# A two-layer graph attention kernel on one core: quarter-width value matmuls, and group ends on ScalarE and in transfers

## The chip, the core and the metric

The kernel runs on one core of a Trainium2 chip. A core has TensorE for matmuls (PE in the profile; its weight loads are PEld), VectorE (DVE), ScalarE (ACT), GpSimd (POOL) and SyncE (SP, which here only issues transfers). SBUF is the memory of the engines, 128 partitions wide; PSUM is where TensorE writes. The metric is the device time of one execution in microseconds (us), lower is better.

## What is computed

The input is x (4096 x 512) and an adjacency matrix adj (4096 x 4096), all in 32-bit floats. Cut to what matters:

```python
# layer 0
h = relu(layernorm(x))
e = (h @ edge_w) @ (h @ edge_w).T                # 4096 x 4096
edge_att = softmax(where(adj > 0, e, -9e15), axis=1)
x = x + adj * (softmax(h @ node_w, axis=0) * edge_att) @ (h @ weight) + bias
# layer 1: 8 heads of 64
h = relu(layernorm(x))
v = (h @ W.T + b).reshape(4096, 8, 64)
e = leaky_relu(src[:, None] + trg[None, :], 0.01) + adj     # for each head; src, trg: sums over v
x = x + (softmax(e, axis=-1) @ v)                # for each head, heads side by side
```

So adj is a mask in layer 0 and an addend to the scores in layer 1.

## The kernel before

**Layer 0** has three passes. The first makes the projections. The second makes the scores e once for each symmetric pair of blocks, writes them to a DRAM scratch e_d and keeps row maxima. The third, around which the change is made, runs over 8 blocks b of 512 output rows and, in each, 32 tiles m of 128 source rows: 256 steps. The order is written out by hand (`manual_schedule`): at each step the functions of a list are called with a lead in steps, `stages = ((load, 8), (turn, 3), (exps, 2), (weigh, 1), (gather, 0))`. Every engine works through its own instructions in the order in which they are written there.

- `load`: SP fetches scores (`et` or `eb`) and adjacency (`a`).
- `turn`: where the stored block is the mirrored one, TensorE transposes it (L271).
- `exps`: VectorE masks and subtracts (L279, L282, L283), ScalarE takes the exponential (L285).
- `weigh`: VectorE multiplies by adj (L291); GpSimd sums the denominators in racc (L301).
- `gather`: four matmuls (L324) add to four PSUM banks po0 to po3, one for each 128 rows of the block. There is one set of these banks.

At m = 0 `gather` also fetches four x tiles through SP and adds the bias on GpSimd (L311). At m = 31 it makes row sums by TensorE (L318), takes the reciprocal on VectorE (L320, L321), and after the last matmuls VectorE reads each po, scales it and adds x (L328); GpSimd's queue stores it to x1 in DRAM (L330).

**Between the layers** a pass over 32 row tiles makes v (`va`), the head projections and four tables of exponentials. The leaky exponential splits so that only a max or a relu of a row vector z and a column factor has to be taken for each pair; z is stored in DRAM (z_d) and read back broadcast to all partitions.

**Layer 1's main loop** runs over 8 groups i: 4 blocks of 1024 output rows (WL) times 2 sets of 4 heads (HG). In each group there are 32 tiles m of 128 source rows, again 256 steps. `stages = ((load, 3), (exps, 1), (weigh, 1), (factors, 2), (gather, 0))`.

- `load`: SP fetches adjacency, tile e, 512 KB; there are three buffers.
- `zload`: a broadcast row of z, 512 KB, on GpSimd's queue. There are six buffers and four z to a group. z3 and z0 are loaded with the first `load` of a group, z1 and z2 with its first `factors`, so at leads of 3 and 2 steps.
- `factors`: ScalarE makes e3 = exp(e + log factor) for head 3 (L474) and rl = relu(...) from z0 (L477).
- `exps`: ScalarE makes ex = exp(e) in PSUM (L465), in one buffer.
- `weigh`: VectorE makes the four products pr of 128 x 1024 in the order k = 3, 0, 1, 2 (L489, and L486 for k = 0). k = 3 uses e3 and the others use ex. GpSimd adds k = 3 to acc3 (L498), and an accumulating transfer adds k = 0 to acc0 or acc1 (L504).
- `gather`: TensorE multiplies values and products (L516) into four PSUM banks pv, two heads in a bank (64 partitions each), and sums the denominators of k = 1 and 2 into the bank dn, in quarters of 32 partitions (L522). An fp32 matmul is two MATMUL and two weight-load instructions in the profile.

At m = 31 ScalarE copies the four pv banks and dn to SBUF (L531, L532). `finish` is a generator: from step 3 of the next group on, one stretch of it runs after each step. It transposes denominators and takes reciprocals (L543, L544), sums acc by matmuls with ones (L553 to L556, copied at L558), and then, for each pair of 128-row tiles, fetches y from x1 through ScalarE's queue (L567), transposes the values (L572), scales and adds them on VectorE (L575, L577, L578) and stores the result through ScalarE's queue (L579).

Of the kernel before, what the change touches and what calls it, by code (L numbers as in the profile page):

```python
# [8 lines left out]
FP = mybir.dt.float32  # L9
AF = mybir.ActivationFunctionType  # L10
ALU = mybir.AluOpType
# [4 lines left out]
P = 128  # L16
# [12 lines left out]
def kernel(  # L29
# [27 lines left out]
    ident = const.tile([P, P], FP, name="ident")  # L57
# [4 lines left out]
    x1 = dram.tile([N, F], FP, name="x1")  # L62
    z_d = dram.tile([H * NT, P], FP, name="z_d")
# [27 lines left out]
    na = big.tile([P, NT], FP, name="na")  # L91
# [128 lines left out]
    with tc.tile_pool(name="c_e", bufs=9) as etp, tc.tile_pool(name="c_b", bufs=4) as ebp, tc.tile_pool(  # L220
# [12 lines left out]
        def rows_of(m):  # L233
            return slice(m * P, (m + 1) * P)
# [69 lines left out]
        def gather(b, m):  # L304
            if m == 0:
                blk[b][2] = [p_o.tile([P, F], FP, name=f"po{j}") for j in range(TB)]
                blk[b][3] = []
                for j in range(TB):
                    xt = iop.tile([P, F], FP, name="xt")
                    nc.sync.dma_start(xt, x[rows_of(b * TB + j), :])  # L310
                    nc.gpsimd.tensor_tensor(xt, xt, bias_b, ALU.add)  # L311
                    blk[b][3].append(xt)
            mb, racc, po, xts = blk[b]
            last = m == NT - 1
            if last:
                rs = p_r.tile([P, TB], FP, name="rs")
                for j in range(TB):
                    nc.tensor.matmul(rs[:, j:j + 1], racc[:, j * P:(j + 1) * P], ones, start=True, stop=True)  # L318
                sc = sp.tile([P, TB], FP, name="sc")
                nc.vector.reciprocal(sc, rs)  # L320
                nc.vector.tensor_tensor(sc, sc, na[:, b * TB:(b + 1) * TB], ALU.mult)  # L321
            w = at.pop((b, m))
            for j in range(TB):
                nc.tensor.matmul(po[j], w[:, j * P:(j + 1) * P], sup[:, m, :], start=(m == 0), stop=last)  # L324
            if last:
                for j in range(TB):
                    ot = iop.tile([P, F], FP, name="ot")
                    nc.vector.scalar_tensor_tensor(ot, po[j], sc[:, j:j + 1], xts[j],  # L328
                                                   op0=ALU.mult, op1=ALU.add)
                    nc.gpsimd.dma_start(x1[rows_of(b * TB + j), :], ot)  # L330

        stages = ((load, 8), (turn, 3), (exps, 2), (weigh, 1), (gather, 0))
        for s in range(-8, len(steps)):
            for f, ahead in stages:
                if 0 <= s + ahead < len(steps):
                    f(*steps[s + ahead])
    l0.close()


# [91 lines left out]
    WL = 1024  # L431
# [3 lines left out]
    with tc.tile_pool(name="e", bufs=3) as ep, tc.tile_pool(name="e3", bufs=2) as e3p, tc.tile_pool(  # L435
# [13 lines left out]
        def load(i, m):  # L449
            b, g = groups[i]  # L450
            e = ep.tile([P, WL], FP, name="e")
            nc.sync.dma_start(e, adj_t[m * P:(m + 1) * P, b * WL:(b + 1) * WL])
            ra[i, m] = e
            if m == 0:
                zload(i, 3)
                zload(i, 0)

        def zload(i, k):
            b, g = groups[i]
            zs_[i, k] = zp.tile([P, WL], FP, name="z")  # L460
            nc.gpsimd.dma_start(zs_[i, k], row_bcast(z_d, WL, (g * HG + k) * N + b * WL))

        def exps(i, m):
            x_ = p_x.tile([P, WL], FP, name="ex")
# [41 lines left out]
        def gather(i, m):  # L506
            b, g = groups[i]
            if m == 0:
                pv[i] = ([[p_v.tile([P, BL], FP, name=f"pv{c}{q}") for q in range(HV)] for c in range(2)],
                         p_v.tile([P, BL], FP, name="dn"))  # L510
            v, dn = pv[i]
            flags = dict(start=(m == 0), stop=(m == NT - 1))
            for c, pair in enumerate(((3, 0), (1, 2))):
                for q in range(HV):
                    for r, k in enumerate(pair):
                        nc.tensor.matmul(v[c][q][r * D:(r + 1) * D, :], va[:, m, g * HG + k, :],  # L516
                                         pr[i, m, k][:, q * BL:(q + 1) * BL], **flags)
            for k in (1, 2):
                d = d_m[:, g * HG + k, m:m + 1]
                for q in range(HV):  # L520
                    r = (k - 1) * 2 + q
                    nc.tensor.matmul(dn[r * Q:(r + 1) * Q, :], d.to_broadcast([P, Q]),  # L522
                                     pr[i, m, k][:, q * BL:(q + 1) * BL], **flags)
            for k in range(HG):
                pr.pop((i, m - 1, k), None)
            if m == NT - 1:
                os_ = [[osp.tile([P, BL], FP, name=f"os{c}{q}") for q in range(HV)] for c in range(2)]
                od = osp.tile([P, BL], FP, name="od")
                for c in range(2):
                    for q in range(HV):  # L530
                        nc.scalar.copy(os_[c][q], v[c][q])  # L531
                nc.scalar.copy(od, dn)  # L532
                late[i] = os_, od

        def finish(i):
            b, g = groups[i]
            os_, od = late.pop(i)
            rd = sp.tile([P, WT, HG], FP, name="rd")

            def dens(src, two):  # L540
                pt = p_t.tile([P, WT // HV, P], FP, name="pt")
                for j in range(WT // HV):
                    nc.tensor.transpose(pt[:, j, :], src[:, j * P:(j + 1) * P], ident)  # L543
                nc.vector.reciprocal(rd[:, :, two].rearrange("p (q j) k -> p j k q", q=HV),  # L544
                                     pt.rearrange("p j (k q d) -> p j k q d", k=2, q=HV)[:, :, :, :, 0])

            dens(od, slice(2, 4))
            yield

            ps = p_t.tile([P, BL], FP, name="pt")  # L550
            for q in range(HV):
                s = slice(q * BL, (q + 1) * BL)
                nc.tensor.matmul(ps[q * Q:(q + 1) * Q, :], ones, acc[i, 3][:, s], start=True, stop=True)  # L553
                r = HV + q
                nc.tensor.matmul(ps[r * Q:(r + 1) * Q, :], ones, acc[i, 0][:, s], start=True, stop=False)
                nc.tensor.matmul(ps[r * Q:(r + 1) * Q, :], ones, acc[i, 1][:, s], start=False, stop=True)  # L556
            oa = osp.tile([P, BL], FP, name="oa")
            nc.scalar.copy(oa, ps)  # L558
            yield
            dens(oa, slice(0, 2))  # L560
            yield
            for j in range(0, WT, 2):
                rows = slice(b * WL + j * P, b * WL + (j + 2) * P)
                y = iop.tile([P, 2, HG, D], FP, name="y")

                cols = slice(g * HG * D, (g + 1) * HG * D)
                nc.scalar.dma_start(y, x1[rows, cols].rearrange("(j p) (h d) -> p j h d", p=P, h=HG))  # L567
                pt = p_t.tile([P, 2, HG, D], FP, name="pt")
                for q in range(2):
                    for c in range(2):  # L570
                        s = (j + q) * P % BL
                        nc.tensor.transpose(pt[:, q, 2 * c:2 * c + 2, :].rearrange("p k d -> p (k d)"),  # L572
                                            os_[c][(j + q) * P // BL][:, s:s + P], ident)
                o = sp.tile([P, 2, HG, D], FP, name="o")
                nc.vector.tensor_tensor(o, pt, rd[:, j:j + 2, :].unsqueeze(3).to_broadcast([P, 2, HG, D]),  # L575
                                        ALU.mult)
                nc.vector.tensor_tensor(y[:, :, 0:3, :], y[:, :, 0:3, :], o[:, :, 1:4, :], ALU.add)  # L577
                nc.vector.tensor_tensor(y[:, :, 3, :], y[:, :, 3, :], o[:, :, 0, :], ALU.add)  # L578
                nc.scalar.dma_start(out[rows, cols].rearrange("(j p) (h d) -> p j h d", p=P, h=HG), y)  # L579
                yield  # L580

        stages = ((load, 3), (exps, 1), (weigh, 1), (factors, 2), (gather, 0))
        for s in range(-3, len(steps)):
            for f, ahead in stages:
                if 0 <= s + ahead < len(steps):
                    f(*steps[s + ahead])
            if s > NT and s % NT == 3:
                ending = finish(s // NT - 1)
            if s > NT and s % NT >= 3:
                next(ending, None)  # L590
        for _ in finish(len(groups) - 1):
            pass
# [34 lines left out]
```

## Time and profile before

| What | Value |
|---|---|
| median of 3 runs | 3289.96 us (3289.59 to 3289.97) |
| the profiled execution | 3290.54 us, span 3288.7 us, granted TensorE clock 0.981 |
| layer 0, first pass | until about 283 us |
| layer 0, second pass | about 284 to 741 us |
| layer 0, third pass (L324) | 760.1 to 1745 us |
| between the layers | 1745 to 1915 us |
| layer 1, main loop | 1915.1 to 3261.2 us |
| after the last product | 3261.2 to 3288.7 us |

The span is counted from the first to the last instruction of the program; the execution's own time has 1.8 us around it. Busy times of an engine are sums within a stretch. A number in brackets behind a line of the timeline is the time that the engine stood idle before it, with the instruction or transfer that ended it.

### The profile page before, as it was taken

The page shows a single profiled execution, that of the slowest core. Times are in us where ns is not written, and L with a number is a line of the kernel's source. Part 1 is how long each engine was busy: PE and PEld are TensorE (multiplying, and loading weights), DVE is VectorE, ACT ScalarE, POOL GpSimd, SP SyncE. Part 2 cuts the span into 40 slices and gives each one's busy share as a digit, 9 for nine tenths or more (in the row PEclk, how much of TensorE's full clock was granted, in tenths as well). Part 3 has the DMA queues.
Part 4 walks back from the last instruction along what each step waited for, and adds up shares of the span by engine and source line. Part 5 has one row for each costly group of instructions (what it writes and reads, how often), then busy time and mean ns, then how long its engine had stood idle before and what let it go on. Part 6 is the DMA issues. An engine that isn't in the chain of part 4 may idle for free.

```text
span 3288.7 us, 34545 instructions
## 1 busy us (share of the span) xinstructions
PE 3117.9 (95%) x11514; PEld 1291.8 (39%) x11514; DVE 2573.5 (78%) x3593; ACT 1195.6 (36%) x1417; POOL 1415.7 (43%) x1081
## 2 busy tenths in 40 slices
PE   8999999998999999999998869999999999999997
PEld 4554444444444444444444423232323232323332
DVE  3324777776667678788896599898989898999997
ACT  2211111111111111111113256565656666666664
POOL 0001111113434445445454546565656565655554
PEclk9999999998999999999999989999999999999999
DMA  2104666656444444454433179898988898989896
GB/s 74 39 20 158 225 219 229 223 182 211 142 141 155 142 157 159 141 163 157 147 107 103 36 188 223 228 218 225 219 224 217 222 223 224 222 227 219 227 221 161
DMA packets 239250, 577.07 MB, mean 175 GB/s; under 512 B 26048, under 2 KB 51936, under 8 KB 239072
## 3 DMA queue, kind: packets, MB, share of 16 engines
q1 hardware_dynamic: 163680, 357.76, 32.7%
q0 software_dynamic: 55680, 196.13, 26.9%
q10 hardware_dynamic: 19712, 20.98, 2.1%
q8 instruction: 90, 1.47, 0.2%
q14 instruction: 88, 0.72, 0.1%
HBM read 389.02 MB, written 51.53 MB: 134 GB/s over the span
## 4 chain that ended last, share of the span: by engine, by line
PE 62%; DVE 18%; issue 6%; ACT 6%; DMA 4%; POOL 2%; ACTq 0%; DVEq 0%; SPq 0%; POOLq 0%
PE po L324 26%; PE pe L180 14%; DVE pr L489 13%; PE pv L516 8%; ACT e L474 5%; PE ps L136 3%; PE pe L129 3%; PE dn L522 2%; DMA z<-z_d 2%; PE pd L382 2%; PE pt L271 2%; DMA y<-x 1%; POOL pr L387 1%; PE lg L139 1%; DVE d L283 1%
## 5 line engine op out<-in xcount | busy, mean ns | idle before, releaser
L516 PE MATMUL pv<-pr,va 128*64 128x512 f32 x4096 | 1025.2, 610 | 61.5 <-DVE pr L489 40.2
L324 PE MATMUL po<-sup,at 128*128 128x512 f32 x2048 | 915.2, 598 | 45.1 <-DVE at L291 45.1
L498 POOL TENSOR_TENSOR acc<-acc,pr 128x1024 f32<-128x1024 f32 x240 | 570.3, 2376 | 434.2 <-DVE pr L489 434.0
L489 DVE SCALAR_TENSOR_TENSOR pr<-z,g_m,ex 128x1024 f32<-128x1024 f32 x512 | 631.4, 1273 | 41.9 <-DMA z<-z_d 41.9
L516 PEld LDWEIGHTS pv<-pr,va 128*64 128x64 f32 x4096 | 359.4, 137 | 686.0 <-issue 378.7
L324 PEld LDWEIGHTS po<-sup,at 128*128 128x128 f32 x2048 | 380.2, 192 | 479.7 <-issue 403.7
L301 POOL TENSOR_TENSOR racc<-racc,ex 128x512 f32<-128x512 f32 x240 | 354.7, 1478 | 467.4 <-ACT ex L285 466.8
L285 ACT ACTIVATE ex<-d 128x512 f32<-128x512 f32 x256 | 161.3, 630 | 829.0 <-DVE d L283 829.0
L180 PE MATMUL pe<-he_t 128*128 128x512 f32 (+3 forms) x1152 | 455.8, 557 | 0.1
L465 ACT ACTIVATE ex<-e 128x1024 f32<-128x1024 f32 x256 | 263.1, 1028 | 456.6 <-DVE pr L489 356.9
L486 DVE SCALAR_TENSOR_TENSOR pr<-rl,gd_m,ex 128x1024 f32<-128x1024 f32 x256 | 326.0, 1274 | 29.1 <-ACT ex L465 29.1
L489 DVE SCALAR_TENSOR_TENSOR pr<-z,g_m,e 128x1024 f32<-128x1024 f32 x256 | 327.6, 1280 | 0.0
L477 ACT ACTIVATE rl<-z,ngd_m,d_m 128x1024 f32<-128x1024 f32 x256 | 314.1, 1227 | 26.9 <-DMA z<-z_d 26.9
L180 PEld LDWEIGHTS pe<-he_t 128*128 128x128 f32 x1152 | 212.9, 190 | 234.5 <-issue 222.5
L474 ACT ACTIVATE e<-e,ld_m 128x1024 f32<-128x1024 f32 x256 | 290.0, 1133 | 5.0 <-DMA z_d<-zs 5.0
L283 DVE TENSOR_TENSOR d<-d,mk 128x512 f32<-128x512 f32 x256 | 273.7, 1069 | 8.8
L522 PE MATMUL dn<-pr,d_m 128*32 128x512 f32 x2048 | 273.8, 607 | 0.0
L184 POOL DMA_DIRECT2D e_d<-es x144 | 79.2, 550 | 351.3 <-ACT es L183 345.8
L282 DVE TENSOR_TENSOR d<-pt,mb 128x512 f32<-128x512 f32 (+2 forms) x136 | 87.4, 643 | 172.6 <-PE pt L271 172.6
L183 ACT COPY es<-pe 128x512 f32<-128x512 f32 (+2 forms) x144 | 79.3, 551 | 376.2 <-PE pe L180 376.2
L504 POOL DMA_DIRECT2D acc<-pr x240 | 208.2, 868 | 5.0 <-DVE pr L486 4.0
L291 DVE TENSOR_TENSOR at<-ex,a 128x512 f32<-128x512 f32 x256 | 190.5, 744 | 0.5
(116 smaller groups left out, 2182.9 us busy)
## 6 DMA issues: line engine op xcount, KB each, us to landing
e<-in_adj_t_dram SPq DMA_DIRECT2D x256, 512.0 KB, 4.5
acc<-pr POOLq DMA_DIRECT2D x256, 512.0 KB, 4.9
a<-in_adj_t_dram SPq DMA_DIRECT2D x256, 256.0 KB, 3.4
ar<-in_adj_dram SPq DMA_DIRECT2D x120, 256.0 KB, 3.1
e_d<-es POOLq DMA_DIRECT2D x120, 256.0 KB, 2.8
ac<-in_adj_t_dram SPq DMA_DIRECT2D x112, 256.0 KB, 3.2
eb<-e_d SPq DMA_DIRECT2D x28, 1024.0 KB, 5.8
et<-e_d SPq DMA_DIRECT2D x112, 256.0 KB, 3.5
```

The costliest lines, as they stand in the source:

```text
L180: nc.tensor.matmul(pe[:, :w], he_t[:, k, rows], he_t[:, k, cols], start=(k == 0), stop=(k == KC - 1))
L283: nc.vector.tensor_tensor(d, d, mk, ALU.add)
L301: nc.gpsimd.tensor_tensor(racc, racc, e, ALU.add)
L324: nc.tensor.matmul(po[j], w[:, j * P:(j + 1) * P], sup[:, m, :], start=(m == 0), stop=last)
L465: nc.scalar.activation(x_, ra.pop((i, m)), AF.Exp)
L474: nc.scalar.activation(x_, ra[i, m], AF.Exp, bias=ld_m[:, h + 3, m:m + 1])
L477: nc.scalar.activation(r, zs_[i, 0], AF.Relu, bias=ngd_m[:, h, m:m + 1], scale=d_m[:, h, m:m + 1])
L486: nc.vector.scalar_tensor_tensor(w, rl.pop((i, m)), gd_m[:, h, m:m + 1], x_, op0=ALU.add, op1=ALU.mult)
L489: nc.vector.scalar_tensor_tensor(w, zs_[i, k], g_m[:, h + k, m:m + 1], e3.pop((i, m)) if k == 3 else x_, op0=ALU.max, op1=ALU.mult)
L498: nc.gpsimd.tensor_tensor(acc[i, 3], acc[i, 3], w, ALU.add)
L516: nc.tensor.matmul(v[c][q][r * D:(r + 1) * D, :], va[:, m, g * HG + k, :], pr[i, m, k][:, q * BL:(q + 1) * BL], **flags)
L522: nc.tensor.matmul(dn[r * Q:(r + 1) * Q, :], d.to_broadcast([P, Q]), pr[i, m, k][:, q * BL:(q + 1) * BL], **flags)
```

## The change

There are five parts.

- **Layer 0, block ends.** The x loads and bias adds move from m = 0 to m = 8. At m = 31 ScalarE copies each po bank to SBUF (`oc`). VectorE's reciprocal and the scale-and-add move into a new `finish`, called once a step after `weigh` in steps 2 to 5 of the next block; it works in place on oc in SBUF.
- **Value matmuls.** Each value matmul of 64 output partitions becomes two of 32, with the same products streamed to both.
- **z loads** move from GpSimd's queue to SP's, and z0 is loaded ahead of z3.
- **Layer 1, group ends.** dn is copied at the first stretch of `finish`, which now runs at step 0 of the next group. Steps 1 and 2 are left out as places for stretches. The copy of the ones-matmuls' sums gets its own stretch.
- **Output of layer 1.** Transposed values go one 128-row tile to a stretch. ScalarE scales each head's 64 columns from PSUM into o with a per-partition factor, in the order of heads. An accumulating transfer on GpSimd's queue adds x1 to o, and a store on SP's queue, one stretch later, writes it to the output. VectorE's three instructions and ScalarE's two transfers are gone.

```diff
@@ layer 0, third pass
             if m == 0:
...
                 blk[b][3] = []
+            if m == TB * 2:
...
             if last:
                 for j in range(TB):
-                    ot = iop.tile([P, F], FP, name="ot")
-                    nc.vector.scalar_tensor_tensor(ot, po[j], sc[:, j:j + 1], xts[j],
-                                                   op0=ALU.mult, op1=ALU.add)
-                    nc.gpsimd.dma_start(x1[rows_of(b * TB + j), :], ot)
+                    oc = iop.tile([P, F], FP, name="oc")
+                    nc.scalar.copy(oc, po[j])
+                    left.append((b * TB + j, oc, rs if j == 0 else None, xts[j]))
+        def finish():
+            t, oc, rs, xt = left.pop(0)
+            b, j = divmod(t, TB)
+            if j == 0:
+                sc = sp.tile([P, TB], FP, name="sc")
+                nc.vector.reciprocal(sc, rs)
+                nc.vector.tensor_tensor(sc, sc, na[:, b * TB:(b + 1) * TB], ALU.mult)
+                scale[b] = sc
+            nc.vector.scalar_tensor_tensor(oc, oc, scale[b][:, j:j + 1], xt, op0=ALU.mult, op1=ALU.add)
+            nc.gpsimd.dma_start(x1[rows_of(t), :], oc)
...
+                if f is weigh and left and s % NT > 1:
+                    finish()
@@ layer 1
+                zload(i, 0)
                 zload(i, 3)
-                zload(i, 0)
...
-            nc.gpsimd.dma_start(zs_[i, k], row_bcast(z_d, WL, (g * HG + k) * N + b * WL))
+            nc.sync.dma_start(zs_[i, k], row_bcast(z_d, WL, (g * HG + k) * N + b * WL))
...
-                        nc.tensor.matmul(v[c][q][r * D:(r + 1) * D, :], va[:, m, g * HG + k, :],
-                                         pr[i, m, k][:, q * BL:(q + 1) * BL], **flags)
+                        for c0 in range(0, D, Q):
+                            nc.tensor.matmul(v[c][q][r * D + c0:r * D + c0 + Q, :],
+                                             va[:, m, g * HG + k, c0:c0 + Q],
+                                             pr[i, m, k][:, q * BL:(q + 1) * BL], **flags)
...
-                nc.scalar.copy(od, dn)
-                late[i] = os_, od
+                late[i] = os_, dn
         def finish(i):
...
+            od = osp.tile([P, BL], FP, name="od")
+            nc.scalar.copy(od, dn)
+            yield
...
+            for t in range(WT + 3):
+                if 0 < t <= WT:
+                    if t % 2:
+                        o = iop.tile([P, 2, HG, D], FP, name="o")
+                    for r, k in enumerate(ORDER):
+                        nc.scalar.activation(o[:, (t - 1) % 2, k, :], pt[:, r, :], AF.Copy,
+                                             scale=rd[:, t - 1, r:r + 1])
+                    if t % 2 == 0:
+                        nc.gpsimd.dma_start(o, part(x1, b * WT + t - 2, cols), accum_op=ALU.add)
+                if t > 2 and t % 2:
+                    nc.sync.dma_start(part(out, b * WT + t - 3, cols), oo)
+                if t % 2 == 0:
+                    oo = o
+                if t < WT:
+                    q, j = divmod(t, WT // HV)
+                    pt = p_t.tile([P, HG, D], FP, name="pt")
+                    for c in range(2):
+                        nc.tensor.transpose(pt[:, 2 * c:2 * c + 2, :].rearrange("p k d -> p (k d)"),
+                                            os_[c][q][:, j * P:(j + 1) * P], ident)
                 yield
...
-            if s > NT and s % NT == 3:
+            if s >= NT and s % NT == 0:
                 ending = finish(s // NT - 1)
-            if s > NT and s % NT >= 3:
+            if s >= NT and s % NT not in (1, 2):
                 next(ending, None)
```

More of the change, by code (lines that the diff above doesn't have):

```diff
@@ L318, in gather @@
                     nc.tensor.matmul(rs[:, j:j + 1], racc[:, j * P:(j + 1) * P], ones, start=True, stop=True)
-                sc = sp.tile([P, TB], FP, name="sc")
-                nc.vector.reciprocal(sc, rs)
-                nc.vector.tensor_tensor(sc, sc, na[:, b * TB:(b + 1) * TB], ALU.mult)
             w = at.pop((b, m))
@@ L326, in gather @@
                 for j in range(TB):
-                    ot = iop.tile([P, F], FP, name="ot")
-                    nc.vector.scalar_tensor_tensor(ot, po[j], sc[:, j:j + 1], xts[j],
-                                                   op0=ALU.mult, op1=ALU.add)
-                    nc.gpsimd.dma_start(x1[rows_of(b * TB + j), :], ot)
+                    oc = iop.tile([P, F], FP, name="oc")
+                    nc.scalar.copy(oc, po[j])
+                    left.append((b * TB + j, oc, rs if j == 0 else None, xts[j]))
+        left, scale = [], {}
+        def finish():
[8 more added lines that the diff above has]
+            nc.gpsimd.dma_start(x1[rows_of(t), :], oc)
         stages = ((load, 8), (turn, 3), (exps, 2), (weigh, 1), (gather, 0))
@@ L336 @@
                     f(*steps[s + ahead])
+                if f is weigh and left and s % NT > 1:
+                    finish()
+        while left:
+            finish()
     l0.close()
@@ L527, in gather @@
                 os_ = [[osp.tile([P, BL], FP, name=f"os{c}{q}") for q in range(HV)] for c in range(2)]
-                od = osp.tile([P, BL], FP, name="od")
                 for c in range(2):
@@ L531, in gather @@
                         nc.scalar.copy(os_[c][q], v[c][q])
-                nc.scalar.copy(od, dn)
-                late[i] = os_, od
+                late[i] = os_, dn
         def finish(i):
             b, g = groups[i]
-            os_, od = late.pop(i)
+            os_, dn = late.pop(i)
+            od = osp.tile([P, BL], FP, name="od")
+            nc.scalar.copy(od, dn)
+            yield
             rd = sp.tile([P, WT, HG], FP, name="rd")
@@ L556, in finish @@
                 nc.tensor.matmul(ps[r * Q:(r + 1) * Q, :], ones, acc[i, 1][:, s], start=False, stop=True)
+            yield
             oa = osp.tile([P, BL], FP, name="oa")
             nc.scalar.copy(oa, ps)
-            yield
             dens(oa, slice(0, 2))
             yield
[L562 to L569, printed above, removed]
-                    for c in range(2):
[L571 to L579, printed above, removed]
@@ new lines, in finish @@
+            cols = slice(g * HG * D, (g + 1) * HG * D)
+            o = None
+            for t in range(WT + 3):
[14 more added lines that the diff above has]
+                    pt = p_t.tile([P, HG, D], FP, name="pt")
+                    for c in range(2):
+                        nc.tensor.transpose(pt[:, 2 * c:2 * c + 2, :].rearrange("p k d -> p (k d)"),
+                                            os_[c][q][:, j * P:(j + 1) * P], ident)
@@ L580, in finish, with part @@
                 yield
+        def part(ap, t, cols):
+            return ap[t * P:(t + 2) * P, cols].rearrange("(j p) (h d) -> p j h d", p=P, h=HG)
         stages = ((load, 3), (exps, 1), (weigh, 1), (factors, 2), (gather, 0))
```

## Prediction

> **What bounds the kernel now.** I read engine shares first, then a table of stretches, then single stretches.
>
> ```profile
> PE 3117.9 (95%) x11514; PEld 1291.8 (39%) x11514; DVE 2573.5 (78%) x3593; ACT 1195.6 (36%) x1417; POOL 1415.7 (43%) x1081
> ```
>
> TensorE looks like the bound, but matmuls are pipelined, so this share settles nothing. The timeline of a quiet stretch of layer 1 (start, length, engine, line):
>
> ```profile
> 2499.60 1.27 DVE L489 SCALAR_TENSOR_TENSOR pr<-z,g_m,ex 128x1024 f32<-128x1024 f32 x1
> 2500.79 1.27 DVE L489 SCALAR_TENSOR_TENSOR pr<-z,g_m,e 128x1024 f32<-128x1024 f32 x1
> 2501.99 1.27 DVE L486 SCALAR_TENSOR_TENSOR pr<-rl,gd_m,ex 128x1024 f32<-128x1024 f32 x1
> ...
> 2503.78 3.85 PE L516 MATMUL pv<-pr,va 128*64 128x512 f32 x16
> 2507.55 1.06 PE L522 MATMUL dn<-pr,d_m 128*32 128x512 f32 x8
> ```
>
> VectorE starts an instruction every 1.192 us and never pauses: four make a step of 4.77 us. TensorE's step has the same 3.77 + 1.00, but catching up after a stall (2287.68 to 2291.26, then 1.00) it needs 3.58 + 1.00 = 4.58. **VectorE bounds the steady step**, with TensorE 0.19 behind. So 32 steps cost 152.6 us. The stretches, one a group (columns: length, PE, PEld, DVE, ACT, POOL busy, clock, DMA share, GB/s):
>
> ```profile
> 1915.10:2069.80 154.70, 153.17 (x752) 52.36 (x753) 154.70 (x129) 101.92 (x95) 100.91 (x66) 0.98 0.88 216
> 2069.80:2239.40 169.60, 164.53 (x807) 52.52 (x805) 159.14 (x144) 106.22 (x102) 101.73 (x68) 0.98 0.90 224
> ```
>
> Group 0 ends nothing and takes 154.7; the seven later ones take 170.2 in the mean, 17.6 over 152.6. Two places hold it. At the boundary:
>
> ```profile
> 2239.35 1.28 DVE L489 SCALAR_TENSOR_TENSOR pr<-z,g_m,e 128x1024 f32<-128x1024 f32 x1
> 2242.13 1.28 DVE L486 SCALAR_TENSOR_TENSOR pr<-rl,gd_m,ex 128x1024 f32<-128x1024 f32 x1 [1.51 <-ACT ex L465]
> 2249.03 2.55 DVE L489 SCALAR_TENSOR_TENSOR pr<-z,g_m,ex 128x1024 f32<-128x1024 f32 x2 [5.61 <-DMA z<-z_d]
> ```
>
> The 1.51 is also z: ScalarE's rl waited for z0 and held ex behind it. Together 7.1 us. And where the old group is finished:
>
> ```profile
> 2294.38 0.68 DVE L575 TENSOR_TENSOR o<-pt,rd 128x512 f32<-128x512 f32 x1
> 2295.09 0.56 DVE L577 TENSOR_TENSOR y<-y,o 128x384 f32<-128x384 f32 x1
> 2295.57 0.28 DVE L578 TENSOR_TENSOR y<-y,o 128x128 f32<-128x128 f32 x1
> ...
> 2297.38 1.28 DVE L486 SCALAR_TENSOR_TENSOR pr<-rl,gd_m,ex 128x1024 f32<-128x1024 f32 x1 [0.33 <-ACT ex L465]
> ```
>
> Work and wait are 1.8 us, four times a group; the rest (oa copy holding ex, reciprocals) is about 3 us.
>
> In layer 0 (steps of 3.43 us, 3.87 with transposes) TensorE is the bound, except where a block ends:
>
> ```profile
> 1135.89 7.11 PE L324 MATMUL po<-sup,at 128*128 128x512 f32 x16
> 1144.83 3.70 PE L324 MATMUL po<-sup,at 128*128 128x512 f32 x8 [1.83 <-DVE at L291]
> 1151.25 1.12 PE L324 MATMUL po<-sup,at 128*128 128x512 f32 x2 [2.72 <-DVE at L291]
> ...
> 1136.07 0.18 DVE L320 RECIPROCAL sc<-rs 128x4 f32<-128x4 f32 x1 [3.46 <-PE rs L318]
> ...
> 1137.09 3.33 DVE L328 SCALAR_TENSOR_TENSOR ot<-po,sc,xt 128x512 f32<-128x512 f32 x4 [0.64 <-PE po L324]
> ```
>
> VectorE, in order, stands 3.46 us before L320, then drains PSUM at TensorE's pace; the masks and weights queued behind come late. TensorE loses 1.83 + 2.72, and some 0.5 in overlap: 5.0 us a boundary. In four of seven it then runs a step at the low clock (5.0 to 5.5 us for 3.4 to 3.9, about 1.8 more). Seven boundaries: 35 + 7 = **42 us**.
>
> **What the Trainium skill says.** "TensorEngine Tiling (Array Packing)", Key Properties: changing the tiling mode drains the array, while different tiles run in parallel. The trace agrees: two quarter waves take 1.00 us to the next mode, where loads of half-width pairs follow at 0.43 (2504.26, 2504.69, 2505.12). "TensorE: Matmul & The Clock Gate", Wait — 56ns, not 53.3ns?: a matmul decoded in microcode costs about 62 ns; no stretch here shows sustained issue that dense. "DMA: Bandwidth & Descriptors", Queues, rings and completion order: each DMA engine takes turns between queue rows. The accumulating row and SP's row do share engines here: 59% and 34% of their time in the steady stretch.
>
> **The change part by part.**
>
> *Layer 0 ends.* Four ScalarE copies from PSUM (0.58 each, as L531) replace VectorE's read; ScalarE works 0.63 of a step, so they fit. Each is queued ahead of the next ex, which moves by at most a gather (3.43) against a lead of two steps. VectorE's reciprocal and four products (0.75) spread over steps 2 to 5: 3.21 + 0.83 = 4.0 against 3.43, 2.4 us taken from that lead. POOL's four stores move with them. SP's four x loads and POOL's four bias adds (1.63) move to step 8. Beside those adds two VectorE steps took some 10 us instead of 6.4 (1141 to 1151), so 3.5 us more of the lead goes. I keep 5 us over all blocks as residue: gain **37** (28 to 42).
>
> *Quarter width.* Value MATMULs and weight loads double to 8192. Four tiles share a wave, as pairs share one now: 8 + 2 waves of 0.43 (third quarter wave at 2276.36 after 2275.93) and no mode switch: 4.34 us a step against 4.58. VectorE hides it wholly: **0** in the steady step. It pays for the transposes: 10 steps have them, and 4.34 + 0.36 (two transposes; four take 0.59) + 0.15 for the switch = 4.85, nearly VectorE's pace; the missing 0.08 fits in the one-step lead. There is one buffer for transposes, so those of a tile wait until ScalarE has scaled the tile before, about 4.1 us into the step; the matmuls of the next step are queued behind them, and end about 4.4 into that step. VectorE needs their buffers (two for k=1 and k=2) only a step later.
>
> *z loads.* 32 issues leave POOL (0.82 each) for SP. z0 and z3 go right behind the e load at 2226.2, some 3 us earlier, z0 first: the 1.5 goes. z1 waits for the slot that the last rl frees (2233.2), z2 for that of the last k=3 product (2235.9), against 2238.93 and 2239.5: 5.7 and 3.5 us earlier. An e load queued behind them has two steps until its use and lands in 4.5, so it can give up 5. A pure shift leaves 3.5 us before z2; their own row should take a little off. But engines were full there (share 1.00 to 1.05 from 2230 to 2245). I take 2.5 (0 to 5.6).
>
> *dn copy.* It goes behind ScalarE's next step. dn of the next group waits some 2 us on TensorE, whose quarter steps regain it; the four os copies (2.0) hold ex about 0.4. The two reciprocals (0.26) stay, plus 0.3 wait for transposes of oa: 1.2 in all.
>
> *Output.* VectorE loses L575, L577, L578 (96 instructions, 48.8 us) and ScalarE 64 DMA issues. ScalarE gets 256 scalings of 128x64: 0.21 us each by extrapolating its copies (128x128 0.266, 128x256 0.373), or 0.12 start to start; 0.35 by "ScalarE: Activation LUTs", Rules for kernel authors. Four fit behind 3.2 us of a 4.77 step even at 0.35. POOL gets 32 accumulating DMAs (0.87 as L504; free time 1.5 a step), SP 32 stores. **SP's store waits until the accumulate has landed**: issued about 4.4 us into a step, landed 5 later, so the next e load, due 5.8 in, leaves near 10 and is needed by e3 at 15.3 with 4.5 to land: slack about 1 us. DMA engines, already 0.93 busy, get some 2.5 us more in two steps (9.54). So I keep 2.5 a group (0 to 9.6, that is 2.4 for each of four).
>
> A later group: 152.6 + 1.2 + 2.5 + 2.5 = 158.8; 7 × 11.4 = **80** gained.
>
> *Tail.* Now 27.5 us after the last product. The accumulates chain: two o buffers, so the third pair waits until the first has been accumulated (4.3) and stored (2.5). I get 29: **+1.5** (-3 to +4).
>
> Sum on the profiled execution (3290.54; span 3288.7 plus 1.8 around it): 3290.5 - 37 - 80 + 1.5 = **3175**. The median of the runs is 0.6 lower, which I ignore.
>
> **Rivals.**
> - *z comes no earlier*, since the engines are full: only the 1.5 goes, 3.1 × 7 = 22 worse: 3197. For: 1.05 share. Against: in 2245 to 2250, 396 GB/s moved as soon as accumulates stopped.
> - *SP becomes the new wait*: 9.6 a group for stores and 4 for z: gain 2.8 × 7 = 20, so 3235. For: the 1 us slack. Against: VectorE's own delays give it time.
> - *Issue bounds TensorE*: 80 instructions × 62 ns (an estimate from the skill's clock-gate page, taking weight loads like matmuls) = 4.96 a step. A group is 158.7 + 4.4 for transposes and ones-matmuls + 2.5 for z = 165.6, group 0 6 more than now: 3290.5 - 37 - 32 + 6 + 1.5 = 3229. It decides from 4.77.
> - *Slower*: a quarter wave of 0.535 (busy 273.8 us over 512 waves of dn) instead of 0.43, so 5.35 a step. A group is 171.2 + 4.4 + 2.5 = 178, group 0 173: 55 + 19 - 36 = 38 more: 3328. It decides from 0.52 a wave. Against: 0.43 seen within a quarter run; that quotient includes fill and drain.
> - *All stalls go*: 3133.
>
> **How the numbers follow.** Chances: forecast 0.64, z 0.12, SP 0.12, issue 0.03, slow waves 0.07, cancelling 0.02. A measurement tells 0.2%, 6.6 us, from no change: faster 0.91, same 0.02, slower 0.07. The range: above, to the SP case; below, half way to no stalls left: 3146 to 3236.
>
> **What would show it.** Right: steady steps still 4.77 with VectorE unbroken; value and dn waves at 0.43; no TensorE wait at L324's block ends; groups near 159; VectorE's wait for z near 2.5. Wrong: steady steps over 4.8; e3 waiting for its e load in steps 8 to 17; ex late behind the scalings; TensorE waiting for weights in layer 0 near step 8.

## The result: 3241.3 us, and the profile after

| | before | after |
|---|---|---|
| median | 3289.78 us (3284.51 to 3289.97) | 3241.30 us (3237.12 to 3246.16) |
| ratio | | 0.9857, 95% interval 0.9837 to 0.9877 |
| profiled execution | 3290.54, span 3288.7 | 3246.16, span 3244.2, clock 0.979 |
| layer 0, third pass, first to last matmul into po | 983.8 | 957.9 |
| first product of layer 1 | at 1915.1 | at 1885.2 |
| first to last product with e3 (k = 3) | 1341.2 | 1320.4 |
| from there to the end | 32.4 | 38.7 |

The change gained 48 us, where the forecast had 115; the end of the range, 3236, was missed by 5. The last three rows make the difference of the two spans: -30.0 - 20.8 + 6.3 = -44.5. Of the 30 us at the first product of layer 1, 26 are the third pass itself; the rest lies before and after it.

The page of the kernel after: the engines' shares, then four of its groups (line, engine, operation, tiles, count | busy in us, mean ns | idle time ahead of it, and what ended most of that).

```profile
PE 3051.1 (94%) x15610; PEld 1229.2 (38%) x15610; DVE 2540.6 (78%) x3497; ACT 1265.5 (39%) x1705; POOL 1426.3 (44%) x1081
...
L532 PE MATMUL pv<-pr,va 128*32 128x512 f32 x8192 | 1090.7, 608 | 55.1 <-DVE pr L504 28.3
L322 PE MATMUL po<-sup,at 128*128 128x512 f32 x2048 | 909.2, 596 | 23.1 <-DVE at L291 23.1
...
L504 DVE SCALAR_TENSOR_TENSOR pr<-z,g_m,ex 128x1024 f32<-128x1024 f32 x512 | 631.4, 1273 | 18.5 <-DMA z<-z_d 17.6
...
L489 ACT ACTIVATE e<-e,ld_m 128x1024 f32<-128x1024 f32 x256 | 291.5, 1139 | 111.3 <-DMA e<-in_adj_t_dram 106.1
```

The shares say almost what they said before. The last column says more: TensorE still waits 23.1 us in layer 0 for VectorE (45.1 before), of which 11.5 (13.4 before) are one wait at the start of the pass; VectorE's wait for z in these products is down to 17.6, and ScalarE's e3 waits 106.1 us for the adjacency tile.

A block end of layer 0, TensorE:

```profile
1232.42 10.46 PE L322 MATMUL po<-sup,at 128*128 128x512 f32 x24
1242.73 0.95 PE L319 MATMUL rs<-ones,racc 128*128 128x1 f32 x8
1243.54 12.69 PE L322 MATMUL po<-sup,at 128*128 128x512 f32 x29
```

No idle time stands behind any of the three: the waits of 1.83 and 2.72 at the block end are gone.

The stretches of layer 1, groups 0, 1 and 2 and the end (columns as before):

```profile
1885.20:2039.70 154.50, 149.08 (x1260) 45.18 (x1260) 154.50 (x130) 102.53 (x95) 99.43 (x63) 0.98 0.89 225
2039.70:2208.00 168.30, 155.88 (x1316) 44.74 (x1316) 153.81 (x132) 112.79 (x134) 104.61 (x68) 0.96 0.91 225
2208.00:2376.00 168.00, 155.53 (x1316) 44.56 (x1316) 153.75 (x132) 112.79 (x134) 104.71 (x68) 0.98 0.92 226
3205.50:3244.20 38.70, 15.91 (x98) 5.46 (x96) 5.40 (x7) 11.95 (x39) 7.91 (x6) 0.68 0.41 81
```

VectorE's work in a later group fell from 159.1 to 153.8, yet the group fell only from 169.6 to 168.3. To see where the rest went I measured each step from one k = 3 product on VectorE to the next, took off 4.77, and averaged over groups 1 to 6. The steps left out, 1 to 3 and 20 to 31, lose 0.6 us at most. Each row is one profiled execution; that of after lies 5 us above its median, some 0.7 a group, so differences below one microsecond in a cell mean little. This table carries the study; the rows below "after" are the experiments.

| us lost in a group | step 0 | 4 to 7 | 8 to 11 | 12 to 19 | whole group |
|---|---|---|---|---|---|
| before | 7.5 | 3.8 | 6.3 | 0.0 | 17.6 |
| **after** | **2.7** | **3.1** | **0.0** | **9.1** | **14.9** |
| late_store | 2.4 | 2.2 | 0.0 | 0.0 | 4.7 |
| bufs3 | 1.8 | 2.7 | 0.0 | 8.8 | 13.4 |
| old_out | 1.6 | 4.5 | 5.9 | 0.0 | 12.5 |
| half | 1.9 | 3.8 | 0.0 | 7.2 | 13.1 |
| late_half | 2.0 | 3.6 | 0.0 | 0.0 | 5.9 |
| z_pool | 8.0 | 1.0 | 0.0 | 7.7 | 16.7 |
| b_quarter | 7.9 | 2.6 | 6.6 | 0.0 | 17.1 |
| spread | 2.8 | 2.6 | 0.0 | 7.9 | 13.4 |
| rec_late | 2.0 | 0.2 | 0.2 | 8.9 | 11.4 |
| best | 2.2 | 0.3 | 0.3 | 0.1 | 3.4 |
| best_z | 0.4 | 0.3 | -0.1 | 0.0 | 1.0 |

VectorE's output work (steps 8 to 11, 6.3 us) is gone, and 9.1 us have come up in steps 12 to 19. There the timelines of group 2 show a chain over three engines. GpSimd issues the accumulate into o, SP stands at the store, and ScalarE waits for e. First GpSimd:

```profile
2263.03 1.41 POOL L592 DMA_DIRECT2D o<-x  x1
...
2272.57 1.44 POOL L592 DMA_DIRECT2D o<-x  x1
```

SP, where an e load (L467) is due every 4.77 us:

```profile
2259.74 0.33 SPq L467 DMA_DIRECT2D e<-in_adj_t_dram  x1
2270.01 0.40 SPq L594 DMA_DIRECT2D out_dram<-o  x1
2270.50 1.04 SPq L467 DMA_DIRECT2D e<-in_adj_t_dram  x2
2281.31 0.40 SPq L594 DMA_DIRECT2D out_dram<-o  x1
2281.80 0.91 SPq L467 DMA_DIRECT2D e<-in_adj_t_dram  x2
```

ScalarE:

```profile
2276.27 1.15 ACT L489 ACTIVATE e<-e,ld_m 128x1024 f32<-128x1024 f32 x1 [2.23 <-DMA e<-in_adj_t_dram]
...
2288.28 1.15 ACT L489 ACTIVATE e<-e,ld_m 128x1024 f32<-128x1024 f32 x1 [3.25 <-DMA e<-in_adj_t_dram]
```

The accumulate of 2263.03 lands after 7 us, at 2270; only then does SP issue the store, and the e load due near 2264.5 leaves at 2270.50, two at once. It lands 5.7 us later, and e3 is 2.23 us late. The next accumulate takes 8.7 us and e3 is 3.25 late.

### The profile page after: what moved, and what is told of

Its sections match the earlier page's. It is cut to its first block, busy times and chain, and to the rows that moved or that the text cites. A ratio compares the mean times of both kernels' runs of the same rounds, so it can differ in the third digit from the quotient of the medians.

```text
span 3244.2 us, 43097 instructions
## 1 busy us (share of the span) xinstructions
PE 3051.1 (94%) x15610; PEld 1229.2 (38%) x15610; DVE 2540.6 (78%) x3497; ACT 1265.5 (39%) x1705; POOL 1426.3 (44%) x1081
## 3 DMA queue, kind: packets, MB, share of 16 engines
q10 hardware_dynamic: 2304, 4.20, 0.4%
## 4 chain that ended last, share of the span: by engine, by line
PE 53%; DVE 18%; DMA 10%; issue 9%; ACT 9%; POOL 1%; SPq 0%; DVEq 0%; POOLq 0%; ACTq 0%
PE po L322 21%; PE pe L180 14%; DVE pr L504 11%; DMA e<-in_adj_t_dram 8%; ACT e L489 6%; PE pv L532 4%; PE ps L136 4%; PE pe L129 3%; PE pd L397 2%; PE pt L271 2%; DVE at L291 2%; PE dn L539 1%; DVE d L282 1%; DMA o<-x 1%; POOL pr L402 1%
## 5 line engine op out<-in xcount | busy, mean ns | idle before, releaser
L532 PE MATMUL pv<-pr,va 128*32 128x512 f32 x8192 | 1090.7, 608 | 55.1 <-DVE pr L504 28.3
L322 PE MATMUL po<-sup,at 128*128 128x512 f32 x2048 | 909.2, 596 | 23.1 <-DVE at L291 23.1
L504 DVE SCALAR_TENSOR_TENSOR pr<-z,g_m,ex 128x1024 f32<-128x1024 f32 x512 | 631.4, 1273 | 18.5 <-DMA z<-z_d 17.6
L532 PEld LDWEIGHTS pv<-pr,va 128*32 128x32 f32 x8192 | 295.6, 111 | 711.1 <-issue 455.0
L301 POOL TENSOR_TENSOR racc<-racc,ex 128x512 f32<-128x512 f32 x240 | 342.9, 1429 | 427.9 <-ACT ex L285 426.1
L539 PE MATMUL dn<-pr,d_m 128*32 128x512 f32 x2048 | 378.5, 598 | 18.4 <-ACT od L556 18.4
L489 ACT ACTIVATE e<-e,ld_m 128x1024 f32<-128x1024 f32 x256 | 291.5, 1139 | 111.3 <-DMA e<-in_adj_t_dram 106.1
L291 DVE TENSOR_TENSOR at<-ex,a 128x512 f32<-128x512 f32 x256 | 191.8, 749 | 21.7 <-ACT ex L285 21.3
```

The source lines that it names most:

```text
L301: nc.gpsimd.tensor_tensor(racc, racc, e, ALU.add)
L489: nc.scalar.activation(x_, ra[i, m], AF.Exp, bias=ld_m[:, h + 3, m:m + 1])
L504: nc.vector.scalar_tensor_tensor(w, zs_[i, k], g_m[:, h + k, m:m + 1], e3.pop((i, m)) if k == 3 else x_, op0=ALU.max, op1=ALU.mult)
L532: nc.tensor.matmul(v[c][q][r * D + c0:r * D + c0 + Q, :], va[:, m, g * HG + k, c0:c0 + Q], pr[i, m, k][:, q * BL:(q + 1) * BL], **flags)
```

## Experiments

**Theories.** A: SP's queue, in order, stands at the store until the accumulate has landed, and the e loads behind it are late. B: the DMA engines are full, and the same bytes would be late in any order. C: two o buffers are too few. The experiments below were timed in three sessions, in which the kernel before had medians of 3287.8 to 3289.9 us, so 2 us between runs of different sessions mean nothing.

**late_store.** The store two stretches later, which needs a third o buffer.

```diff
-                        o = iop.tile([P, 2, HG, D], FP, name="o")
+                        o = iop.tile([P, 2, HG, D], FP, name="o", bufs=3)
...
-                if t > 2 and t % 2:
-                    nc.sync.dma_start(part(out, b * WT + t - 3, cols), oo)
+                if t > 4 and t % 2:
+                    nc.sync.dma_start(part(out, b * WT + t - 5, cols), os2.pop(0))
```

> The changed kernel with one edit: each output store on SP's queue comes two stretches (two steps) later, with a third buffer for o, so that the accumulate has landed before SP reaches the store. Theory A, SP's queue: the e loads stand behind a store that waits for the accumulate; without that wait steps 12 to 19 of a group lose at most 2 us instead of about 9, ScalarE's wait for e falls from 106 to under 45 us, and the kernel takes 3241 - 45 to 55 = about 3190. Theory B, full DMA engines: the accumulates and e loads are late because 16 engines are busy, whatever the order; then steps 12 to 19 still lose 6 us or more and the time stays over 3220.

Measured: 3174.52 us, ratio to before 0.9657 (0.9641 to 0.9673), 67 us less than after. SP in group 2:

```profile
2251.50 5.10 SPq L467 DMA_DIRECT2D e<-in_adj_t_dram  x2
2258.60 0.40 SPq L595 DMA_DIRECT2D out_dram<-o  x1
...
```

5.10 for two issues: they are 4.77 apart again. Steps 12 to 19 lose nothing, and ScalarE's wait for e, in the table of waits, goes to

```profile
ACT e L489 <- DMA e<-in_adj_t_dram: 9.1, 9, 2.5
```

Against B speaks the table of transfers (KB, median us from issue to landing), for some 40 us around the outputs of group 2, first of after (2262 to 2304), then of late_store (2252 to 2292):

```profile
acc<-pr POOLq DMA_DIRECT2D x8, 512.0 KB, 8.1
e<-in_adj_t_dram SPq DMA_DIRECT2D x6, 512.0 KB, 7.2
o<-x POOLq DMA_DIRECT2D x4, 256.0 KB, 9.1
```

```profile
e<-in_adj_t_dram SPq DMA_DIRECT2D x8, 512.0 KB, 7.1
out_dram<-o SPq DMA_DIRECT2D x4, 256.0 KB, 5.7
o<-x POOLq DMA_DIRECT2D x3, 256.0 KB, 9.1
```

The transfers are as slow in the kernel without the stall, and the DMA engines are no less busy there (share 1.07 in this stretch, 1.00 in after). An e load of 7.1 us does no harm if it leaves on time. So order, not bandwidth, sets the loss. I had expected 3190, since I did not trust so full a set of DMA engines to take it all.

**bufs3.** The third buffer without the later store, since late_store changed both.

```diff
-                        o = iop.tile([P, 2, HG, D], FP, name="o")
+                        o = iop.tile([P, 2, HG, D], FP, name="o", bufs=3)
```

> The later store of the kernel with the store two stretches later came with a third o buffer, so this is the third buffer alone, with the store where the changed kernel has it. Theory A: the loss of some 9 us a group in steps 12 to 19 comes from SP's queue standing in front of the store until the accumulate has landed; a third buffer takes nothing away from that, so the time stays within 10 us of the changed kernel's 3241 (3232 to 3245; a few us may go in the tail, where the third pair waited for the first one's store). ScalarE's wait for e stays near 106 us. Rival: the loss was a wait for o buffers, and the third buffer alone is the gain: near 3175, with the wait for e near 10.

Measured: 3231.87 us (3227.67 to 3237.09), 9 less than after. ScalarE's wait for e stays, and steps 12 to 19 lose 8.8:

```profile
ACT e L489 <- DMA e<-in_adj_t_dram: 105.1, 40, 6.7
```

C falls: the place of the store is worth 57 of the 67 us. Of the 9, some 3 are the end (38.7 to 35.3); the rest is spread over the groups and not traced further.

**old_out.** The output of layer 1 as before, all else as changed.

```diff
-                        nc.scalar.activation(o[:, (t - 1) % 2, k, :], pt[:, r, :], AF.Copy,
-                                             scale=rd[:, t - 1, r:r + 1])
...
+                nc.scalar.dma_start(y, x1[rows, cols].rearrange("(j p) (h d) -> p j h d", p=P, h=HG))
...
...
+                nc.vector.tensor_tensor(o, pt, rd[:, j:j + 2, :].unsqueeze(3).to_broadcast([P, 2, HG, D]),
+                                        ALU.mult)
...
```

> The changed kernel with the output as before: y through ScalarE's queue, scale and add on VectorE (L575, L577, L578 of before), stores through ScalarE's queue; all else as changed. The output part alone is undone. If theory A or B holds, the output part gained VectorE 6.1 us and ScalarE's waits a group but gave back about 9: then this kernel, at 4 x 1.8 = 7.2 us a group, is within 15 us of 3241 (3230 to 3250). If the output part was a gain after all (the loss in steps 12 to 19 comes from z or from quarter-width issue), it is slower, about 3241 + 7 x 7 = 3290.

Measured: 3224.47 us, ratio 0.9807 (0.9793 to 0.9822), a little below the span expected. As it was changed, the output part **costs** 17 us: it removes some 7 us in steps 4 to 11 and puts 9.1 in steps 12 to 19, and its end is longer (38.7 against 30.9). Around the outputs of group 2 of old_out (2236 to 2276) the loads also land as fast as in the kernel before:

```profile
e<-in_adj_t_dram SPq DMA_DIRECT2D x6, 512.0 KB, 4.5
y<-x ACTq DMA_DIRECT2D x4, 256.0 KB, 3.5
```

So it is the new output that brings e to 7.2.

**half and late_half.** Value matmuls of 64 columns again, first in after, then in late_store.

```diff
-                        for c0 in range(0, D, Q):
-                            nc.tensor.matmul(v[c][q][r * D + c0:r * D + c0 + Q, :],
-                                             va[:, m, g * HG + k, c0:c0 + Q],
-                                             pr[i, m, k][:, q * BL:(q + 1) * BL], **flags)
+                        nc.tensor.matmul(v[c][q][r * D:(r + 1) * D, :], va[:, m, g * HG + k, :],
+                                         pr[i, m, k][:, q * BL:(q + 1) * BL], **flags)
```

> The changed kernel with value matmuls of 64 columns again. If VectorE alone sets the steady step, as predicted, the steady step stays at 4.77; but TensorE then needs 4.58 + 0.36 + mode switch in steps with transposes and catches up 0.19 a step instead of 0.43 after a boundary, so the waits for od and oa transposes (steps 4 and 6) grow from 1.2 to about 2.5 each and the kernel takes 3241 + 15 to 25 = about 3260. If quarter width gives nothing, it stays within 5 us of 3241; if quarter width costs something (issue, weight loads), this kernel is faster than 3235.

> The late-store kernel with value matmuls of 64 columns. In the changed kernel both widths took the same time, where stalls in steps 12 to 19 could hide a difference. Without those, quarter width is worth what it saves at the waits for od and oa transposes (0.4 to 1.5 us in steps 4 and 6), some 1.3 a group, plus any lag of TensorE in steps 7 to 15 (4.58 + 0.36 + 0.15 = 5.1 a step against 4.77, 8 steps, 2.6 us, of which a step's lead can hide most): 3174.5 + 10 to 20. If it stays within 3 us, quarter width is worth nothing here either.

Measured: half 3241.51 us (3239.80 to 3247.26), no different from after, which I had not expected; late_half 3185.1 us, ratio 0.9687 (0.9671 to 0.9703), 10.6 slower than late_store. In both, steps 4 to 7 lose more (3.8 for 3.1, and 3.6 for 2.2): after a stall TensorE needs 4.58 us a step in place of 4.30, so it is further behind when VectorE's reciprocals need its transposes. Both steps stand in the chains of group 2, first of half (3.58 + 0.99), then of after (2228.67 to 2232.97):

```profile
2216.85 3.58 PE pv L531 x16
2220.43 0.99 PE dn L537 x8
```


```profile
2228.67 3.43 PE pv L532 x32
2232.11 0.86 PE dn L539 x8
2232.97 3.43 PE pv L532 x32
```

With the store in the way, steps 12 to 19 of half then lost 1.9 less. That a product made later finds its e tile less late is my reading; no run isolates it.

**b_quarter.** Quarter width alone, in the kernel before.

> The kernel before with quarter-width values alone. VectorE bounds the steady step (4.77), so it stays; TensorE's faster recovery shortens only the waits after a boundary and in the finishing steps (5.17 a step of TensorE before becomes 4.9, but VectorE needs 6.58 there). Expected: no change within 5 us of the kernel before (3283 to 3290). If TensorE were the bound of the steady step, 0.2 x 256 = 50 us less; if issue of 80 instructions a step were the bound, 50 us more.

Measured: 3284.12 us against 3289.9, ratio 0.9982 (0.9975 to 0.9989). The steady step stays 4.77: VectorE bounds it. Steps 4 to 7 lose 2.6 where they lost 3.8, the one column with a gain.

**z_pool.** z loads on GpSimd's queue in the old order.

```diff
             if m == 0:
+                zload(i, 3)
                 zload(i, 0)
-                zload(i, 3)
...
-            nc.sync.dma_start(zs_[i, k], row_bcast(z_d, WL, (g * HG + k) * N + b * WL))
+            nc.gpsimd.dma_start(zs_[i, k], row_bcast(z_d, WL, (g * HG + k) * N + b * WL))
```

> The changed kernel with the z loads back on GpSimd's queue, z3 ahead of z0. If the z loads on SP gave what the step table shows (boundary step 12.2 before, 7.5 now), it is slower by 7 x 4.7 = 33: about 3274. If another part shortened the boundary (dn copy moved, quarter width), it stays within 10 us of 3241. If z ahead of e on SP's row also delays e, part of the gain is given back at steps 0 and 1 and it is slower by only 15 to 25.

Measured: 3264.66 us, ratio 0.9935 (0.9919 to 0.9952), 23 slower than after. VectorE's waits at a boundary, of z_pool, then of after, where the one shown is the worst of seven (4.8 us; the others 0.9 to 3.2):

```profile
2044.26 1.28 DVE L501 SCALAR_TENSOR_TENSOR pr<-rl,gd_m,ex 128x1024 f32<-128x1024 f32 x1 [2.30 <-ACT ex L480]
2051.15 2.56 DVE L504 SCALAR_TENSOR_TENSOR pr<-z,g_m,ex 128x1024 f32<-128x1024 f32 x2 [5.61 <-DMA z<-z_d]
```

```profile
2213.14 1.28 DVE L504 SCALAR_TENSOR_TENSOR pr<-z,g_m,ex 128x1024 f32<-128x1024 f32 x1 [2.68 <-DMA z<-z_d]
2216.34 1.28 DVE L504 SCALAR_TENSOR_TENSOR pr<-z,g_m,ex 128x1024 f32<-128x1024 f32 x1 [1.91 <-DMA z<-z_d]
```

SP's queue saves 5.3 us at step 0, 37 in seven groups. By the table, steps 4 to 7 give 2.1 back and steps 12 to 19 another 1.4, so that 1.8 a group are left, some 13 in seven. That in z_pool TensorE catches up while VectorE waits for z is my reading. The profiled executions lie 18 us apart, the medians 23: the end is 2.9 longer in z_pool, and the profiled execution of after lies above its median.

**spread.** Layer 0's x loads and bias adds one at a time.

```diff
-            if m == TB * 2:
-                for j in range(TB):
+            if m >= TB * 2 and m % TB == 0 and m < TB * 6:
+                for j in (m // TB - 2,):
```

> Only the bias adds of layer 0 (with their x loads), one each at m = 8, 12, 16 and 20 in place of four in a row at m = 8. Theory: the four adds in a row slow VectorE, and TensorE's step of 5.9 at m = 9 is their price, so that layer 0 ends 13 to 15 us earlier and layer 1 keeps its length: 3226 to 3230. Rival: the loss at m = 9 is the four x loads on SP's queue that delay the masks, or it comes back as four small losses: no more than 5 us gained, 3236 to 3241.

Measured: 3226.58 us, ratio 0.9812 (0.9797 to 0.9827), 14.7 less than after; the third pass takes 943.7 for 957.9, though the first product of layer 1 comes only 11.5 us earlier. In the table of waits, TensorE's waits for VectorE go, but for the one at the start of the pass (11.5 and 10.9); the numbers are us in total, times and the longest, first of after, then of spread:

```profile
PE po L322 <- DVE at L291: 23.1, 7, 11.5
```

```profile
PE po L322 <- DVE at L291: 11.9, 2, 10.9
```

The trace of after beside the adds in block 4, GpSimd, then VectorE, then TensorE:

```profile
1275.11 6.46 POOL L312 TENSOR_TENSOR xt<-xt,bias_b 128x512 f32<-128x512 f32 x4
1281.53 3.38 POOL L301 TENSOR_TENSOR racc<-racc,ex 128x512 f32<-128x512 f32 x2
```

```profile
1282.04 1.75 DVE L291 TENSOR_TENSOR at<-ex,a 128x512 f32<-128x512 f32 x1
1283.71 1.48 DVE L279 TENSOR_SCALAR mk<-a 128x512 f32<-128x512 f32 x1
...
1286.43 0.68 DVE L291 TENSOR_TENSOR at<-ex,a 128x512 f32<-128x512 f32 x1
1287.04 0.42 DVE L279 TENSOR_SCALAR mk<-a 128x512 f32<-128x512 f32 x1
```

```profile
1283.84 12.69 PE L322 MATMUL po<-sup,at 128*128 128x512 f32 x25 [2.29 <-DVE at L291]
```

While GpSimd works without a pause (four adds, then the two denominator sums that they had put off), VectorE's instructions take 1.75 and 1.48 us; once it stops, 0.68 and 0.42. Two steps of VectorE take 6.42 (from 1275.62 to 1282.04) and 4.39 so, which uses up the rest of its lead, and TensorE stands 2.29. "SBUF — State Buffer", in its section on SBUF's two separate sides, says that VectorE, in an instruction with two SBUF inputs or in a two-port mode, and GpSimd share a pair of ports that one instruction holds to its end, while the other is blocked. The durations fit: beside adds of 6.46 / 4 = 1.6 us, each of VectorE's grows by 1.06 or 1.07. No run here shows the ports themselves. The x loads moved with the adds, so that spread alone doesn't part the two, but no mask waited for a transfer there.

**rec_late.** Each reciprocal one stretch after the transposes that it reads.

```diff
-            dens(od, slice(2, 4))
+            pt = turned(od)
             yield
+            dens(pt, slice(2, 4))
...
```

> Only the two reciprocals a group one stretch later than the transposes that they read. Theory A: the changed kernel loses some 3 us a group in steps 4 and 6 by VectorE waiting for those transposes; they go to 4.8 to 5.0 each, and ScalarE's wait for e in steps 12 to 19 stays: 7 times 3 gives 3220, or less of a gain if a part comes back in steps 12 to 19, since the e loads there are then needed earlier: 3220 to 3236. Rival: as for the half-width values, all comes back: 3241 within 3.

Measured: 3221.85 us, ratio 0.9800 (0.9785 to 0.9814), 19 less than after. The same reciprocal in after, then in rec_late:

```profile
2237.88 0.26 DVE L564 RECIPROCAL rd<-pt 128x16 f32<-128x16 f32 x1 [1.18 <-PE pt L563]
```

```profile
2234.43 0.26 DVE L567 RECIPROCAL rd<-pt 128x16 f32<-128x16 f32 x1
```

Steps 4 to 7 lose 0.2 for 3.1, which is the whole gain, 20 us in seven groups.

**best and best_z.** late_store with spread and rec_late; then, besides, z0 and z3 of the next group loaded with the e tile of m = 24.

```diff
-            if m == 0:
-                zload(i, 0)
-                zload(i, 3)
+            n = i + (m == 24)
+            if (i, m) == (0, 0) or m == 24 and n < len(groups):
+                zload(n, 0)
+                zload(n, 3)
```

> The late-store kernel with two more edits. (1) Layer 0: x loads and bias adds one tile at a time, at m = 8, 12, 16 and 20, instead of four at m = 8. (2) Layer 1: the two reciprocals run one stretch after their transposes. Theory: the 2.45 us step at m = 9 of blocks 3 to 7 (and the low-clock step after it) is VectorE held beside four bias adds in a row, and spread they fit: layer 0's pass ends 13 to 16 us earlier. Steps 4 and 6 lose 1.0 and 1.6 us, because VectorE waits for transposes behind a lagging TensorE; a step later they are there: 0.2 each remain, 7 x 2.2 = 15 less. So 3174.5 - 29 = about 3146. Rival: TensorE's lag only moves to another wait (p_t has one buffer, ones-matmuls come later): then 3155 to 3160.

> As the run 'best', with z0 and z3 of the next group fetched with e of m = 24 instead of with the next group's first e, so five steps... eight steps earlier. Theory: the boundary still loses 2.3 us because four z loads and the e loads share one row, so that z1 and z2 and the first e come late; with two of them out of the way the boundary loses about 0.5 and it takes 8 to 12 us less than 'best'. Rival: the loss at the boundary is ex behind the os copies and TensorE's wait for dn; then it stays within 3 us of 'best'.

Measured: best 3152.37 us, ratio 0.9580 (0.9566 to 0.9595), between what the two theories gave: 89 us less than after, where the three repairs, each measured alone, gave 101. One reason stands in the table: in late_store steps 4 to 7 lose 2.2, not 3.1, so that there is less for rec_late to repair. best_z 3139.42 us, ratio **0.9545** (0.9531 to 0.9559), 13 less again and the fastest of all. A later group takes 153.6 there, 1.0 over VectorE's own pace. What is left on top is the end, 35 us.

## Why the prediction was wrong

The direction and most of the mechanisms held; one term of the group's sum failed by far, and three others were too small. The profiled execution is 71 us over the forecast: output 46 (6.6 in each of seven groups), group ends 13, layer 0 7, end 5. Two of the signs that I had named for being wrong came: e3 waiting for its e load, and TensorE waiting in layer 0 near step 8. The lower end of the range holds a slip: half way from 3175 to 3133 is 3154, not 3146.

- **The failed step: Output, 2.5 us a group, measured 9.1.** The sentence was right: SP's store waits until the accumulate has landed. Its sizes were not. I let the accumulate land in 5 us and the e load in 4.5, with 1 us of slack. In the stall shown, the first took 7.0 and the second 5.7: 2.0 + 1.2 - 1 = 2.2 us late, and 2.23 was measured. The landing times came from the kernel before, whose transfers were faster (its own table of transfers, 2262 to 2304):

```profile
e<-in_adj_t_dram SPq DMA_DIRECT2D x8, 512.0 KB, 4.3
acc<-pr POOLq DMA_DIRECT2D x7, 512.0 KB, 4.7
y<-x ACTq DMA_DIRECT2D x4, 256.0 KB, 3.8
```

 The change turns y's 3.8 us into an accumulate's 9.1, and the loads beside it slow down; old_out, with y back, has them at 4.5 again. With DMA engines 0.93 busy I should have let landing times grow, not only added 2.5 us of work. My 5 us hold for an accumulate without others beside it: at the end of the kernel o takes 4.1 to 5.0. In the groups it stands behind the accumulate into acc that the same queue has just issued, and lands 1.3 to 1.7 us after that one. "DMA: Bandwidth & Descriptors", Queues, rings and completion order, has the engines take turns between queue rows: in this stretch the accumulating row takes 61.7% of their time and SP's 37.1%, where the kernel before had 52.9 and 24.2. That fits an e load that lands at 7.2 instead of 4.3; no run takes the row alone. The rival "SP becomes the new wait" named this, at 9.6 a group and 3235, with a chance of 0.12. The argument I set against it, that VectorE's own delays give SP time, failed: the change had just taken away those of steps 8 to 11.
- **Group ends.** 1.2 predicted for the dn copy, reciprocals and the wait for transposes; 3.1 measured. TensorE's lag after the boundary makes the transposes later than I had counted (1.18 us in the line above). rec_late shows it.
- **z loads.** 2.5 predicted, 2.7 measured at step 0. The number was right. z1 and z2 do wait for their slots, but what is lost is mostly the crowd of four z loads: in best and best_z alike z1 and z2 leave 6.2 and 3.5 us before the group's first product, at every boundary. In best they land 7.7 to 10.4 us later and 2.2 us are lost; in best_z, where z0 and z3 are there by then, they land 5.7 to 8.1 us later and 0.4 are lost.
- **Quarter width.** Right in the steady step (4.77, by b_quarter as well), and for TensorE's own pace: a step with two transposes was put at 4.85 and takes 4.80 (2248.83 to 2253.63 in after), without them 4.30 against 4.34. What I called 0 "in the steady step" has its worth in catching up, 10.6 us in late_half, and nothing as changed.
- **Layer 0.** -37 predicted, -30 measured at the first product of layer 1, -26 in the pass itself. The waits at the block ends went wholly, but of the 42 us 16 came back instead of 5, at m = 9 and in the slow step behind it. I had counted 2.4 us off VectorE's lead for the finishing and 3.5 for the adds. The adds took 4.0 (steps of 6.42 and 4.39 against 3.43), near enough. But the six steps behind a block end took 5.6: 5.40, 4.41, 4.45, and 3.98 three times. The first of them is a wait that I had bounded and then left out of the sum, ex behind the copies of po on ScalarE:

```profile
1248.40 0.69 DVE L291 TENSOR_TENSOR at<-ex,a 128x512 f32<-128x512 f32 x1 [3.05 <-ACT ex L285]
```

 The waits of VectorE for ex are the same in spread (21.3 us in seven), and TensorE doesn't wait there: so it was the four adds in a row at m = 8, on a lead that the six steps had shortened, that cost the time.
- **Group 0** was put at no change: 154.5 against 154.7.
- **End.** +1.5 predicted, +6.3 measured. The accumulates and stores chain as I said, but the copies, transposes and scalings between them are serial too:

```profile
3224.22 0.93 ACT L589 ACTIVATE o<-pt,rd 128x64 f32<-128x64 f32 x4 [0.78 <-PE pt L601]
3229.15 0.93 ACT L589 ACTIVATE o<-pt,rd 128x64 f32<-128x64 f32 x4 [4.00 <-DMA out_dram<-o]
```

 The 4.00 is the third pair waiting for the first's buffer, and bufs3 took some 3 of it away.

Put together with the measured terms, a later group is 152.6 + 2.7 + 3.1 + 9.1 = 167.5; the trace has 167.3 in the mean of seven.

late_store, which differs from the change by the place of one store, came out at 3174.52, within a microsecond of the forecast. That is partly luck: it gains more in the groups than I counted and less in layer 0 and at the end.

## What to carry to other kernels

A queue that issues in order is an engine with its own critical path: before a transfer that waits for another's landing is put in front of time-critical loads, price that landing under the load of the changed kernel, and give the wait a place late enough to be over when the queue gets there. When a queue, VectorE and TensorE run within a few per cent of one another, freeing one moves the wait: judge each part by a table of loss per step, since the whole time hid a gain of 10 us (half, seen in late_half) and a loss of 17 (old_out). And when several small costs are taken from one lead, add them up in the order in which they come.

## What the runs showed of the hardware that I had not expected

- Beside a long accumulating stream, a 256 KB accumulate into SBUF in packets of 1 KB lands 9.1 us after its issue (median of four), while the same accumulate alone, at the end of the kernel, takes 4.1 to 5.0, and a plain 256 KB fetch took 3.8 in the kernel before.
- With the DMA engines fully busy (share 1.07) and medians of 5.7 to 9.1 us from issue to landing, steps 12 to 19 of late_store lose nothing, since each load leaves on time.
- Four scalings of 128 x 64 in a row on ScalarE take 0.90 to 0.93 us: each is 0.29 to 0.34 long, and they start 0.19 to 0.21 apart. Of my estimates, 0.12, 0.21 and 0.35, the middle one fits what a scaling adds to the row.
- VectorE's instructions of 0.42 to 0.68 us took 1.48 to 1.75 while GpSimd added tiles without a pause. The trace of before shows the same beside its adds. I had counted 3.5 us for two steps; against the same 6.4 they took 4.4.
